# Inverse deviations by Newton steps, a normalization split between two engines, and three re-ordered steps in a four-layer graph kernel

## The chip, the cores and the metric

The kernel runs on one core of one Trainium2 chip, in a single launch. The metric is the device time of that launch in microseconds (us); lower is better. Only fp32 data takes part in the matrix products; the edge mask between layers is kept in bf16.

## The reference

Four graph layers follow each other on x (4096 x 256) and a weighted adjacency matrix adj (4096 x 4096). Every layer ends in the same residual normalization.

```python
def _layernorm(x, axis=-1, eps=1e-5):
    m = jnp.mean(x, axis=axis, keepdims=True)
    v = jnp.var(x, axis=axis, keepdims=True)
    return (x - m) / jnp.sqrt(v + eps)

x = _layernorm(x + L0(x, adj, adj, ...))   # 4-head attention, adj as bias and as mask
x = _layernorm(x + L1(x, adj, ...))        # graph attention: leaky_relu(e_src + e_dst), masked softmax, @ (x W)
x = _layernorm(x + L2(x, adj, ...))        # (D^-1/2 adj D^-1/2 x) W2^T + b2
x = _layernorm(x + L3(x, adj, ...))        # relu((D^-1/2 adj D^-1/2 x) W3)
```

The change touches how 1 / sqrt(v + eps) is formed after layer 0, how the last rows of layer 3 are normalized and stored, and the order of some steps at the start and the end of layer 0.

## The kernel before, in words

All stages stand in one function, `tile_gnn`, and nearly all of it is under a manual schedule: instructions of one engine run in the order in which the Python code issues them, and semaphores tie the engines together. So the order of the code is the order of each engine's queue. 128 rows make a chunk; there are 32 of them.

**Start of layer 0** (L709 to L734). SP and ScalarE issue the loads. SP: the first 512 columns of x transposed (`load_x(0)`, in two halves), `fetch` (what the first queries need), `load_x(1)`, four pieces of raw adjacency for `rows[0].load(0)`, four for `rows[0].load(1)`, then `load_x(2..4)`. ScalarE: weights and biases. `warm` (L209) keeps TensorE busy; `project_k(0)` (L215) makes the first 512 keys as two products, one per pair of heads, in the PSUM banks `po0` and `po1`, each summed over two halves of the feature axis (cc) and moved to SBUF by ScalarE (L228). `rows[0].begin("po1")` (L323) makes the first 128 queries in bank `po1`, and VectorE moves them (L338). Then `project_k(1)`, and the first masks: `make_bias` on VectorE turns raw adjacency (L287) and makes a bias of it (L292, L293). The first three of the steps below also carry the rest of the keys and values: `plan[t]` holds `project_v` (L235; its result lies in the PSUM tile `tr`, moved by VectorE at L248), `project_k` and `first_bias`.

**Layer 0, step by step** (`step(t)`, L501). A unit is one pair of heads of one row chunk: 64 units of NS = 4 steps, each step 1024 keys wide. In a step TensorE does the scores of step t into the two PSUM tiles `sc[0]`, `sc[1]` (L383); VectorE adds the bias, takes the maximum and writes z (L392); ScalarE makes exponentials four steps later (L408); TensorE turns them into the PSUM tile `tr` (L422); ScalarE copies them out (L430, in the last steps half of them by VectorE at L428); TensorE multiplies by the values (L440). `sc` and `tr` are single-buffered, so the next scores wait for L392 and the next turning waits for the copy. At a unit's end VectorE scales (`scale`, L491) with a row that went through a DRAM round trip on GpSimd's queue (`sums` L463, `spread` L484), or, for the last unit, through TensorE (L474); `finish` (L348) multiplies by the output weights (L352), adds the residual (L362) and takes the row statistics (L117, L118).

**The tail of layer 0** is hung on the last steps by the table `tail` (L663), n0 being the step eight before the end of the scores (nd). At n0 + 2 `ln_rstd(0, 30)` (L120) forms the inverse deviations of the 30 finished chunks: VectorE adds eps, ScalarE takes Sqrt, VectorE takes the reciprocal. `norm_part(j)` (L606) normalizes the j-th eighth of the rows on VectorE (L126) and stores it with a DMA of GpSimd's queue (L612). `turn_part(j)` (L616) turns an eighth of x with eight transposes into `sc[0]` and `sc[1]` (L622) and copies each out, cc = 0 by ScalarE (L625) if `split`, else by VectorE (L627). `project_ed` (L630) and `project_w` (L134) make the projections of layer 1. At nd + 7 `last_rstd` (L650) does the last two chunks.

**Layers 1 to 3.** Layer 1 (`gat_step`, L915) multiplies at L891. Layers 2 and 3 share `Block`: seven products per pair of chunks (L1059) in place of eight. The very last block ends in `end` (L1116): eight row groups n = 0 to 7 in two halves h of NSJ = 4; `weigh` multiplies by the weights (L1090), `onto_x` applies Relu on ScalarE (L1142) and adds to x (L1144; GpSimd for n = 0 to 4 and 6, VectorE for 5 and 7), `stats` takes the statistics on VectorE, and `put(h)` (L1151) forms the inverse deviations of the half, normalizes its four groups and stores them with two DMAs. `put(0)` stands before the loop over n = 4 to 7, so its four normalizations come ahead of that loop's VectorE work.

Of the kernel before, what the change touches and what calls it, by code (L numbers as in the profile page):

```python
# [9 lines left out]
BF16 = mybir.dt.bfloat16  # L10
AF = mybir.ActivationFunctionType
# [5 lines left out]
P = 128  # L17
# [19 lines left out]
EPS = 1e-5  # L37
WARM = 8
# [7 lines left out]
def tile_gnn(  # L46
# [38 lines left out]
    sel = const.tile([P, NCH], F32, name="sel")  # L85

# [38 lines left out]
    def ln_apply(dst, src, ci, engine=nc.vector):  # L125
        engine.tensor_scalar(  # L126
            dst, src, mv[:, ci, 0:1], rstd[:, ci : ci + 1], ALU.subtract, ALU.mult
        )
# [43 lines left out]
    with ExitStack() as l0:  # L172
# [42 lines left out]
        def project_k(mb):  # L215

            xt = x_in[mb]
            for pr in range(2):
                pk = ps_o.tile([P, 512], F32, tag=f"po{pr}", name="pk")
                for cc in range(2):  # L220
                    nc.tensor.matmul(  # L221
                        pk,
                        wkv_sb[:, cc, pr * P : (pr + 1) * P],
                        xt[:, cc, :],
                        start=(cc == 0),
                        stop=(cc == 1),
                    )
                nc.scalar.activation(  # L228
                    kT[:, pr, mb * 512 : (mb + 1) * 512],
                    pk,  # L230
                    AF.Identity,
                    bias=bqk_sb[:, 2 + pr : 3 + pr],
                )
# [23 lines left out]
        class Rows:  # L257
# [65 lines left out]
            def begin(self, tag):  # L323
                self.qT = wk2.tile([P, 2, P], F32, tag="qT", name="qT")
                pq = ps_o.tile([P, 512], F32, tag=tag, name="pq")
                for pr in range(2):
                    for cc in range(2):
                        for j in range(2):
                            h = 2 * pr + j
                            nc.tensor.matmul(  # L330
                                pq[j * HD : (j + 1) * HD, pr * P : (pr + 1) * P],
                                wq_sb[:, cc, h * HD : (h + 1) * HD],
                                self.xq[:, cc, :],
                                start=(cc == 0),
                                stop=(cc == 1),
                            )
# [164 lines left out]
        def step(t):  # L501
# [33 lines left out]
            if grow:  # L535
                if pr == 1 and k == NS - 3:
                    rows[ib + 1].begin(tag_o if attends else "po1")
# [77 lines left out]

        def turn_part(j, split=False):  # L616
            xs = parts.pop(j)
            xt = zp.tile([P, 2, NSB, NA, QB], F32, tag="z", name="xt1")
            for cc in range(2):
                px = sc[cc][:, 0:512].rearrange("p (a i) -> p a i", i=P)  # L620
                for a in range(NA):
                    nc.tensor.transpose(px[:, a, :], xs[:, a, cc * P : (cc + 1) * P], ident)  # L622
                to, px = xt[:, cc, :, :, :], px.rearrange("p a (b r) -> p b a r", r=QB)
                if split and cc == 0:
                    nc.scalar.copy(to, px)  # L625
                else:
                    nc.vector.tensor_copy(to, px)  # L627
            turned_x[j] = xt
# [21 lines left out]
        def last_rstd():  # L650
# [15 lines left out]
            n0 + 2: [(load_part, 2), (weight, 1, 1), (ln_rstd, 0, NCH - 2)],  # L666
# [9 lines left out]
            nd + 5: [(turn_part, 5, True)],  # L676
# [32 lines left out]
        with tc.manual_schedule():  # L709
# [11 lines left out]
            nc.scalar.dma_start(bv_b, bv.partition_broadcast(P))  # L721
            rows[0].load(1)
            for mb in range(2, 5):
# [5 lines left out]
            rows[0].begin("po1")  # L729
# [270 lines left out]
    with ExitStack() as l2:  # L1000
# [31 lines left out]
        class Block:  # L1032
# [83 lines left out]
            def end(self, t0):  # L1116
# [7 lines left out]
                py = {}  # L1124

# [25 lines left out]
                def put(h, engines):  # L1151
                    c0 = h * NP + self.jb * NSJ
                    ln_rstd(c0, c0 + NSJ)
                    ob = wk.tile([P, NSJ, D], F32, tag="ob", name="ob", bufs=2)
                    for s in (0, 1, 3, 2):
                        ln_apply(ob[:, s, :], xc[:, c0 + s, :], c0 + s, engines[s])
                    for s, queue in ((0, nc.sync), (2, (nc.sync, nc.scalar)[h])):
                        queue.dma_start(
                            out[(c0 + s) * P : (c0 + s + 2) * P, :].rearrange(
                                "(s p) e -> p s e", p=P  # L1160
                            ),
                            ob[:, s : s + 2, :],
                        )

# [24 lines left out]
                put(0, [nc.vector] * NSJ)  # L1189
# [6 lines left out]
                put(1, [nc.vector] * (NSJ - 1) + [nc.gpsimd])  # L1196
# [114 lines left out]
```

## Time and profile before

| what | value |
|---|---|
| time of the launch, median of 3 runs | 2694.16 us (2693.48 to 2695.2) |
| the profiled execution: its own time | 2693.25 us |
| its span, first to last instruction | 2691.5 us |
| TensorE clock granted, mean | 0.999 |
| TensorE busy | 2670.8 us |
| VectorE busy | 2189.5 us |
| ScalarE busy | 1638.3 us |
| GpSimd busy | 384.2 us |
| DMA | 312.31 MB, mean 116 GB/s |

Busy time by stretch of the span, in us:

| stretch | TensorE | VectorE | ScalarE | GpSimd |
|---|---|---|---|---|
| 0 to 75, start of layer 0 | 71.68 | 42.96 | 23.45 | 10.95 |
| 75 to 1300, layer 0 | 1224.80 | 1112.49 | 1171.47 | 325.01 |
| 1300 to 1345, its last steps | 42.87 | 34.14 | 40.37 | 10.61 |
| 1345 to 1410, into layer 1 | 60.55 | 43.73 | 42.46 | 6.20 |
| 1410 to 1858, layer 1 | 447.85 | 383.22 | 297.83 | 3.28 |
| 1858 to 2672, layers 2 and 3 | 813.55 | 561.94 | 58.82 | 22.30 |
| 2672 to 2691.5, the end | 9.53 | 10.98 | 3.88 | 5.82 |

A timeline line of the profile reads: start in us from the span's start, time in us, engine, source line, operation, output<-input, shape, count; in square brackets the idle time of the engine just before it and what ended that. PE is TensorE's matrix products, PEld its weight loads, DVE VectorE, ACT ScalarE, POOL GpSimd, SP SyncE; a q behind an engine's name is its queue, that issues DMAs.

### The profile page before, as it was taken

The numbers are of one execution on the slowest core, as the hardware profiler recorded it, in microseconds if no ns is written. First come the engines' busy times: TensorE is split into PE (matmuls) and PEld (weight loads), VectorE is DVE, ScalarE is ACT, GpSimd is POOL, SyncE is SP. The second block draws the span as 40 slices with busy tenths as digits, with TensorE's granted clock in tenths as the row PEclk, the third lists the DMA queues.
The fourth block names the chain that finished last, engine by engine and source line by source line (L and its number), as shares of the span: only waits on it lengthen the run. The fifth ranks groups of instructions, "written<-read, shape, count | busy, mean of one in ns | idle before, by whom it ended". The sixth has DMA issues, their size and how long they took to land.

```text
span 2691.5 us, 59102 instructions
## 1 busy us (share of the span) xinstructions
PE 2670.8 (99%) x23858; PEld 1835.5 (68%) x23858; DVE 2189.5 (81%) x4122; ACT 1638.3 (61%) x2677; POOL 384.2 (14%) x665
## 2 busy tenths in 40 slices
PE   9999999999999999999999999999999999999998
PEld 5777777777777777777778888886444444444444
DVE  5999999999999999999769988886966578676675
ACT  2899999999999999999967666672100001000000
POOL 1232232232222222222200000001200000000000
PEclk9999999999999999999999999999999999999999
DMA  7444444444444444444372222222544545455543
GB/s 157 93 94 95 91 93 97 90 93 97 90 91 99 90 92 97 89 94 97 109 219 79 72 78 77 73 79 73 177 157 163 171 157 172 156 168 176 177 162 107
DMA packets 679699, 312.31 MB, mean 116 GB/s; under 512 B 553504, under 2 KB 584096, under 8 KB 679424
## 3 DMA queue, kind: packets, MB, share of 16 engines
q1 hardware_dynamic: 655968, 264.97, 39.1%
q0 software_dynamic: 21504, 41.98, 4.3%
q8 instruction: 187, 3.06, 0.5%
q10 hardware_dynamic: 1952, 1.58, 0.2%
q14 instruction: 88, 0.72, 0.1%
HBM read 262.34 MB, written 46.07 MB: 115 GB/s over the span
## 4 chain that ended last, share of the span: by engine, by line
PE 96%; issue 1%; DMA 1%; ACT 1%; DVE 1%; SPq 0%; POOL 0%; POOLq 0%; DVEq 0%; ACTq 0%
PE m L1059 29%; PE po L440 17%; PE sc L383 17%; PE po L891 17%; PE ptr L422 11%; PE py L1090 2%; PE pq L330 1%; PE pp L352 1%; PE pv L241 1%; PE pk L221 1%; DMA wkv_sb<-in_wqkv 0%; DMA x<-xs 0%; SPq L271 0%; DMA mk<-edge 0%; DMA xt<-in_xT 0%
## 5 line engine op out<-in xcount | busy, mean ns | idle before, releaser
L392 DVE CUSTOM_DVE_ANT_0 z<-sc,bias 128x1024 f32<-128x1024 f32 x512 | 606.1, 1221 | 46.8 <-PE sc L383 46.7
L408 ACT ACTIVATE z<-z,nm 128x1024 f32<-128x1024 f32 x512 | 590.4, 1153 | 0.0
L430 ACT COPY pt<-ptr 128x1024 f32<-128x1024 f32 x507 | 510.5, 1007 | 65.4 <-PE ptr L422 64.6
L440 PE MATMUL po<-pt,xc 128*64 128x128 f32 x8192 | 504.1, 276 | 0.5 <-DVE pt L428 0.5
L383 PE MATMUL sc<-store,qT 64*128 64x512 f32 x2048 | 502.8, 604 | 0.1
L440 PEld LDWEIGHTS po<-pt,xc 128*64 128x64 f32 x8192 | 442.1, 137 | 18.1 <-DVE pt L428 0.8
L891 PE MATMUL po<-store,pt 128*128 128x257 f32 x2048 | 445.6, 379 | 0.0
L422 PEld LDWEIGHTS ptr<-ident,z 64*128 64x128 f32 x8192 | 322.9, 138 | 179.6 <-issue 87.7
L891 PEld LDWEIGHTS po<-store,pt 128*128 128x128 f32 x2048 | 387.3, 189 | 57.6
L422 PE MATMUL ptr<-ident,z 64*128 64x64 f32 x8192 | 356.7, 225 | 3.5 <-ACT pt L430 2.0
L1059 PE MATMUL m<-asum,ysum 128*128 128x512 f32 x672 | 324.7, 592 | 0.0
L383 PEld LDWEIGHTS sc<-store,qT 64*128 64x128 f32 x2048 | 194.0, 188 | 115.5 <-issue 109.6
L1059 PEld LDWEIGHTS m<-asum,ysum 128*128 128x128 f32 x672 | 127.7, 190 | 160.3 <-issue 139.7
L310 POOL DMA_DIRECT2D edge<-mk x256 | 143.1, 559 | 556.1 <-ACT mk L304 540.0
L1023 DVE TENSOR_TENSOR asum<-a,a 128x512 f32<-128x512 f32 x128 | 88.1, 688 | 150.9 <-PE m L1059 150.9
L1059 PE MATMUL m<-asum,store 128*128 128x512 f32 x448 | 210.5, 592 | 0.0
L1059 PE MATMUL m<-a,ysum 128*128 128x512 f32 x448 | 210.5, 592 | 0.0
L293 DVE SCALAR_TENSOR_TENSOR bias<-rt,gb,u 128x512 f32<-128x512 f32 x256 | 194.2, 759 | 9.1
L881 DVE STREAM_TRANSPOSE pt<-z 128x1024 f32<-128x1024 f32 x128 | 158.0, 1236 | 39.5 <-PE po L891 38.3
L1065 ACT COPY e<-m 128x512 f32<-128x512 f32 x28 | 16.2, 585 | 277.4 <-PE m L1059 277.4
L287 DVE STREAM_TRANSPOSE rt<-raw 128x512 f32<-128x512 f32 x256 | 180.0, 703 | 5.1 <-DMA raw<-in_adjT 4.8
L304 ACT ACTIVATE mk<-rt 128x512 bf16<-128x512 f32 x256 | 158.0, 617 | 6.5 <-DMA edge<-mk 3.5
(155 smaller groups left out, 2657.7 us busy)
## 6 DMA issues: line engine op xcount, KB each, us to landing
a<-in_adjT SPq DMA_DIRECT2D x256, 512.0 KB, 4.8
raw<-in_adjT SPq DMA_DIRECT2D x512, 128.0 KB, 3.9
edge<-mk POOLq DMA_DIRECT2D x256, 128.0 KB, 2.5
mk<-edge SPq DMA_DIRECT2D x256, 128.0 KB, 2.9
xq<-in_xT SPq DMA_DIRECT2D x32, 128.0 KB, 3.7
xr<-in_x SPq DMA_DIRECT2D x32, 128.0 KB, 3.0
x<-xs POOLq DMA_DIRECT2D x8, 512.0 KB, 6.5
xc<-x SPq DMA_DIRECT2D x8, 512.0 KB, 5.9
```

The costliest lines, as they stand in the source:

```text
L287: nc.vector.transpose(rt.rearrange("p (b r) -> p b r", r=QB), self.raw_now[:, half * nb : (half + 1) * nb, :],)
L293: nc.vector.scalar_tensor_tensor(self.bias[k][:, m0 : m0 + HT], rt, gb, u, ALU.mult, ALU.add)
L304: nc.scalar.activation(mk, rt, AF.Copy, accum_out=self.rs[:, j : j + 1])
L383: nc.tensor.matmul(ps[j][:, q * 512 : (q + 1) * 512], self.rows.qT[j * HD : (j + 1) * HD, self.pr, :], kT[j * HD : (j + 1) * HD, self.pr, ...
L392: nc.vector.tensor_tensor_reduce(z, ps[j], self.rows.bias[k], 1.0, NEG, ALU.add, ALU.max, self.mx[:, j, k : k + 1],)
L408: nc.scalar.activation(z, z, AF.Exp, bias=self.nm[:, j : j + 1], accum_out=self.ls[:, j, k : k + 1],)
L422: nc.tensor.transpose(pa[:, r, c, :], z[half, c * P : (c + 1) * P], ident[half, half])
L430: nc.scalar.copy(to, pa)
L440: nc.tensor.matmul(self.po[j * HD : (j + 1) * HD, 0:P], v_sb[:, ci, h * HD : (h + 1) * HD], self.pt[j][k][:, c, :], start=(ci == 0), stop= ...
L881: nc.vector.transpose(self.pt[:, :, s, :], self.z[s].rearrange("p (b r) -> p b r", r=QB))
L891: nc.tensor.matmul(self.po[:, 0 : D + 1], self.pt[:, b, :, :].rearrange("p s i -> p (s i)"), wh[:, b, :], start=(b == 0), stop=(b == NBK - 1),
L1059: nc.tensor.matmul(self.m[i], left, right, start=(c == 0), stop=(c == NP - 1))
```

## The change

The change has four parts.

1. **Start.** `project_k` takes both PSUM tiles at once, and for the first 512 keys sums the first half of the features for both pairs of heads before the second half. The first queries lie in `tr` instead of `po1`. `load_x(2)` is issued ahead of `rows[0].load(1)`.
2. **Newton.** For the 30 chunks at n0 + 2, ScalarE's Sqrt and VectorE's reciprocal give way to `ln_newton`: three VectorE instructions (eps, and a first guess made with integer arithmetic on the bits), then four Newton steps of four GpSimd instructions each, all on 128 x 30 values.
3. **Sixth part of x.** `turn_part(5, split)` at nd + 5 becomes two halves: cc = 0, copied by ScalarE, at nd + 4, and cc = 1, copied by VectorE, at nd + 6. Both come last in their step.
4. **End.** `put` is taken apart. `rates(h)` forms the inverse deviations and also -mean / deviation. Of half 0, groups 0, 1 and 3 are normalized by ScalarE (Identity with scale and bias) and group 2 by VectorE, after the loop over n = 4 to 7 instead of before it; of half 1, group 3 by ScalarE and 0 to 2 by VectorE. GpSimd normalizes nothing any more.

```diff
-    def ln_apply(dst, src, ci, engine=nc.vector):
-        engine.tensor_scalar(
+    def ln_newton(c0, c1):
+        n = c1 - c0
+        v, y = newton[:, 0, 0:n], rstd[:, c0:c1]
+        t = newton[:, 1, 0:n]
+        nc.vector.tensor_scalar(v, mv[:, c0:c1, 1], EPS, None, ALU.add)
+        nc.vector.tensor_scalar(
+            y.bitcast(I32), v.bitcast(I32), 1, None, ALU.arith_shift_right
+        )
+        nc.vector.tensor_scalar(
+            y.bitcast(I32), y.bitcast(I32), -1, MAGIC, ALU.mult, ALU.add
+        )
+        for _ in range(4):
+            nc.gpsimd.tensor_tensor(t, y, y, ALU.mult)
+            nc.gpsimd.tensor_tensor(t, t, v, ALU.mult)
+            nc.gpsimd.tensor_scalar(t, t, 0.5, 1.5, ALU.mult, ALU.subtract)
+            nc.gpsimd.tensor_tensor(y, y, t, ALU.mult)
+    def ln_apply(dst, src, ci):
+        nc.vector.tensor_scalar(
             dst, src, mv[:, ci, 0:1], rstd[:, ci : ci + 1], ALU.subtract, ALU.mult
...
+            pk = [ps_o.tile([P, 512], F32, tag=f"po{pr}", name="pk") for pr in range(2)]
+            both = [(pr, cc) for pr in range(2) for cc in range(2)]
+            for pr, cc in both if mb else sorted(both, key=lambda i: i[1]):
+                nc.tensor.matmul(
+                    pk[pr],
+                    wkv_sb[:, cc, pr * P : (pr + 1) * P],
+                    xt[:, cc, :],
+                    start=(cc == 0),
+                    stop=(cc == 1),
+                )
             for pr in range(2):
-                pk = ps_o.tile([P, 512], F32, tag=f"po{pr}", name="pk")
-                for cc in range(2):
-                    nc.tensor.matmul(
-                        pk,
-                        wkv_sb[:, cc, pr * P : (pr + 1) * P],
-                        xt[:, cc, :],
-                        start=(cc == 0),
-                        stop=(cc == 1),
-                    )
                 nc.scalar.activation(
                     kT[:, pr, mb * 512 : (mb + 1) * 512],
-                    pk,
+                    pk[pr],
                     AF.Identity,
                     bias=bqk_sb[:, 2 + pr : 3 + pr],
...
-            def begin(self, tag):
+            def begin(self, pq):
                 self.qT = wk2.tile([P, 2, P], F32, tag="qT", name="qT")
...
-                pq = ps_o.tile([P, 512], F32, tag=tag, name="pq")
...
-                    rows[ib + 1].begin(tag_o if attends else "po1")
+                    rows[ib + 1].begin(
+                        ps_o.tile([P, 512], F32, tag=tag_o if attends else "po1", name="pq")
+                    )
...
+        def turn_half(j, cc, by_act):
+            if cc == 0:
+                turned_x[j] = zp.tile([P, 2, NSB, NA, QB], F32, tag="z", name="xt1")
+            xs = parts.pop(j) if cc else parts[j]
+            px = sc[cc][:, 0:512].rearrange("p (a i) -> p a i", i=P)
+            for a in range(NA):
+                nc.tensor.transpose(px[:, a, :], xs[:, a, cc * P : (cc + 1) * P], ident)
+            to = turned_x[j][:, cc, :, :, :]
+            px = px.rearrange("p a (b r) -> p b a r", r=QB)
+            if by_act:
+                nc.scalar.copy(to, px)
+            else:
+                nc.vector.tensor_copy(to, px)
         def turn_part(j, split=False):
-            xs = parts.pop(j)
-            xt = zp.tile([P, 2, NSB, NA, QB], F32, tag="z", name="xt1")
             for cc in range(2):
-                px = sc[cc][:, 0:512].rearrange("p (a i) -> p a i", i=P)
-                for a in range(NA):
-                    nc.tensor.transpose(px[:, a, :], xs[:, a, cc * P : (cc + 1) * P], ident)
-                to, px = xt[:, cc, :, :, :], px.rearrange("p a (b r) -> p b a r", r=QB)
-                if split and cc == 0:
-                    nc.scalar.copy(to, px)
-                else:
-                    nc.vector.tensor_copy(to, px)
-            turned_x[j] = xt
+                turn_half(j, cc, split and cc == 0)
...
-            n0 + 2: [(load_part, 2), (weight, 1, 1), (ln_rstd, 0, NCH - 2)],
+            n0 + 2: [(load_part, 2), (weight, 1, 1), (ln_newton, 0, NCH - 2)],
...
-            nd + 5: [(turn_part, 5, True)],
+            nd + 4: [(turn_half, 5, 0, True)],
+            nd + 6: [(turn_half, 5, 1, False)],
...
+            load_x(2)
             rows[0].load(1)
-            for mb in range(2, 5):
+            for mb in range(3, 5):
                 load_x(mb)
             nc.scalar.dma_start(wout_sb, wout.rearrange("(c p) e -> p c e", p=P))
             nc.scalar.dma_start(bout_b, bout.partition_broadcast(P))
             warm()
             project_k(0)
-            rows[0].begin("po1")
+            rows[0].begin(ps_t.tile([P, TS], F32, tag="tr", name="pq"))
             project_k(1)
...
+                nmr = wk.tile([P, 2, NSJ], F32, tag="nmr", name="nmr", bufs=1)
+                obs = [wk.tile([P, NSJ, D], F32, tag="ob", name="ob", bufs=2) for h in range(2)]
...
-                def put(h, engines):
-                    c0 = h * NP + self.jb * NSJ
-                    ln_rstd(c0, c0 + NSJ)
-                    ob = wk.tile([P, NSJ, D], F32, tag="ob", name="ob", bufs=2)
-                    for s in (0, 1, 3, 2):
-                        ln_apply(ob[:, s, :], xc[:, c0 + s, :], c0 + s, engines[s])
-                    for s, queue in ((0, nc.sync), (2, (nc.sync, nc.scalar)[h])):
-                        queue.dma_start(
-                            out[(c0 + s) * P : (c0 + s + 2) * P, :].rearrange(
-                                "(s p) e -> p s e", p=P
-                            ),
-                            ob[:, s : s + 2, :],
+                def apply(h, s, by_act):
+                    ci = h * NP + self.jb * NSJ + s
+                    if by_act:
+                        nc.scalar.activation(
+                            obs[h][:, s, :],
+                            xc[:, ci, :],
+                            AF.Identity,
+                            bias=nmr[:, h, s : s + 1],
+                            scale=rstd[:, ci : ci + 1],
                         )
+                    else:
+                        ln_apply(obs[h][:, s, :], xc[:, ci, :], ci)
+                def put(h, s, queue):
+                    c0 = h * NP + self.jb * NSJ + s
+                    queue.dma_start(
+                        out[c0 * P : (c0 + 2) * P, :].rearrange("(s p) e -> p s e", p=P),
+                        obs[h][:, s : s + 2, :],
+                    )
+                def rates(h, between=()):
+                    cs = slice(h * NP + self.jb * NSJ, h * NP + (self.jb + 1) * NSJ)
+                    r = rstd[:, cs]
+                    nc.vector.tensor_scalar(r, mv[:, cs, 1], EPS, None, ALU.add)
+                    nc.scalar.activation(r, r, AF.Sqrt)
+                    for args in between:
+                        apply(*args)
+                    nc.vector.reciprocal(r, r)
+                    nc.vector.scalar_tensor_tensor(
+                        nmr[:, h, :], mv[:, cs, 0], -1.0, r, ALU.mult, ALU.mult
...
-                put(0, [nc.vector] * NSJ)
+                rates(0)
                 for n in range(NSJ, 2 * NSJ, 2):
                     for i in range(n, n + 2):
                         weigh(i, None, (1,))
                         onto_x(i)
                     stats(n)
                     stats(n + 1)
-                put(1, [nc.vector] * (NSJ - 1) + [nc.gpsimd])
+                apply(0, 0, True)
+                apply(0, 1, True)
+                put(0, 0, nc.sync)
+                rates(1, ((0, 2, False), (0, 3, True)))
+                put(0, 2, nc.sync)
+                for s in (3, 0, 1, 2):
+                    apply(1, s, s == 3)
+                put(1, 0, nc.sync)
+                put(1, 2, nc.scalar)
```

More of the change, by code (lines that the diff above doesn't have):

```diff
@@ L10 @@
 BF16 = mybir.dt.bfloat16
+I32 = mybir.dt.int32
 AF = mybir.ActivationFunctionType
@@ L37 @@
 EPS = 1e-5
+MAGIC = 0x5F3759DF
 WARM = 8
@@ L85, in tile_gnn @@
     sel = const.tile([P, NCH], F32, name="sel")
+    newton = const.tile([P, 2, NCH], F32, name="newton")
     x0_pre = dram.tile([N, D], F32, name="x0_pre")
@@ L1149, in stats @@
                     ln_stats(wk, xc[:, ci, :], ci)
-                def put(h, engines):
-                    c0 = h * NP + self.jb * NSJ
-                    ln_rstd(c0, c0 + NSJ)
-                    ob = wk.tile([P, NSJ, D], F32, tag="ob", name="ob", bufs=2)
-                    for s in (0, 1, 3, 2):
-                        ln_apply(ob[:, s, :], xc[:, c0 + s, :], c0 + s, engines[s])
-                    for s, queue in ((0, nc.sync), (2, (nc.sync, nc.scalar)[h])):
-                        queue.dma_start(
-                            out[(c0 + s) * P : (c0 + s + 2) * P, :].rearrange(
-                                "(s p) e -> p s e", p=P
-                            ),
-                            ob[:, s : s + 2, :],
-                        )
+                def apply(h, s, by_act):
[7 more added lines that the diff above has]
+                            scale=rstd[:, ci : ci + 1],
+                        )
+                    else:
[16 more added lines that the diff above has]
+                        nmr[:, h, :], mv[:, cs, 0], -1.0, r, ALU.mult, ALU.mult
+                    )
                 products(2)
```

## The prediction, on record before the run

> **What bounds the kernel now.** I read the page's busy times and its chain of waits first, then the chain in order of time, then the timeline of the four places that the change touches. From the page:
>
> ```profile
> span 2691.5 us, 59102 instructions
> ...
> PE 2670.8 (99%) x23858; PEld 1835.5 (68%) x23858; DVE 2189.5 (81%) x4122; ACT 1638.3 (61%) x2677; POOL 384.2 (14%) x665
> ...
> PE 96%; issue 1%; DMA 1%; ACT 1%; DVE 1%; SPq 0%; POOL 0%; POOLq 0%; DVEq 0%; ACTq 0%
> ```
>
> TensorE is the bound nearly everywhere, and the change takes no product away. It can only win where TensorE stands still or where the end hangs on other engines. The chain leaves TensorE in the first 21 us, around 1316 to 1321, 1366 to 1410, and after 2678. What is saved there goes through to the end, since TensorE's work from one place to the next stays.
>
> Start, from the timeline:
>
> ```profile
> 9.97 1.09 PE L330 MATMUL pq<-xq,w_sb 128*64 128x128 f32 x16 [0.78 <-ACT store L228]
> ...
> 16.55 0.71 DVE L287 STREAM_TRANSPOSE rt<-raw 128x512 f32<-128x512 f32 x1 [4.82 <-DMA raw<-in_adjT]
> ...
> 21.45 3.70 PE L221 MATMUL pk<-xt,wkv_sb 128*128 128x512 f32 x8 [1.18 <-DMA xt<-in_xT]
> ...
> 22.82 1.22 DVE L248 TENSOR_TENSOR xc<-pv,bv_b 128x1024 f32<-128x1024 f32 x1
> ...
> 24.99 3.62 PE L241 MATMUL pv<-wkv_sb,xt 128*128 128x256 f32 x16
> ```
>
> Read two queues here. TensorE waits for ScalarE before the first queries and for the third block of x at 21.45. VectorE waits for raw adjacency until 16.55 and is then busy without a gap until 24.04, when L248 has emptied `tr`; only then may the values at 24.99 be written.
>
> Newton's place (n0 + 2), same view:
>
> ```profile
> 1307.37 0.44 POOL L308 TENSOR_TENSOR mk<-mk,off_diag 128x128 bf16<-128x128 bf16 x1
> ...
> 1307.89 0.43 POOL L309 TENSOR_TENSOR mk<-mk,ident 128x128 bf16<-128x128 bf16 x1
> ...
> 1316.38 1.28 ACT L122 ACT_TABLE_LOAD   x1
> ...
> 1317.92 1.28 ACT L408 ACT_TABLE_LOAD   x1
> ...
> 1320.62 1.37 DVE L126 TENSOR_SCALAR xs<-xs,mv,rstd 128x256 f32<-128x256 f32 x4
> ...
> 1321.40 0.71 PE L422 MATMUL ptr<-ident,z 64*128 64x64 f32 x16 [1.99 <-ACT pt L430]
> ```
>
> Sqrt and the way back to Exp cost ScalarE two table loads; its copy L430 is late, and TensorE stands 1.99 us.
>
> The sixth part of x:
>
> ```profile
> 1366.36 1.96 PE L440 MATMUL po<-pt,xc 128*64 128x128 f32 x30 [0.54 <-DVE pt L428]
> ...
> 1369.99 0.28 DVE L491 TENSOR_TENSOR oT<-po,rb 128x128 f32<-128x128 f32 x1
> ...
> 1370.42 1.08 PE L352 MATMUL pp<-wout_sb,oT 128*64 128x256 f32 x8 [1.07 <-DVE rowsum L359]
> ```
>
> The last values are done at 1368.3, but the scaling L491 sits on VectorE behind the copy L627 (1369.38 to 1370.07), which itself waits for eight transposes.
>
> The end:
>
> ```profile
> 2685.86 0.17 DVE L121 TENSOR_SCALAR rstd<-mv 128x4 f32<-128x4 f32 x1
> ...
> 2686.59 1.39 POOL L126 TENSOR_SCALAR ob<-xc,mv,rstd 128x256 f32<-128x256 f32 x1 [4.04 <-DVE rstd L123]
> ...
> 2688.01 0.40 ACTq L1158 DMA_DIRECT2D out_x<-ob  x1
> ```
>
> GpSimd's 1.39 us normalization releases the last store; ahead of that, VectorE was the only engine with work.
>
> **What the Trainium skill says.** "ScalarE: Activation LUTs", What ACT_TABLE_LOAD costs, gives about 1283 ns for a load plus a drain of about 1380 ns. The trace agrees with the load (1.28 us) and shows no drain: Sqrt starts at 1317.67, as its load ends. The same page, Table sets, says that cheap functions (identity among them) are in every set, so ScalarE's Identity beside Sqrt and Relu at the end should load nothing; before, Relu and Sqrt alternate there without a load. "GPSIMD Engine Reference", Elementwise — side-by-side cycle accounting, has 2.6 cycles per element for a two-input operation; L1144 takes 0.725 us (median) for 256 values and L309 0.43 for 128, or 2.3 ns per value and about 0.14 us fixed (different types, so an estimate). "Perfetto Trace Analysis", GPSIMD Engine Instruction, advises start-to-start spacing for that engine: L308 to L309, which depends on it, is 0.52 us, 0.09 more than the duration.
>
> **Part 1, start.** The reordered first keys fill the waits for the second halves: eight passes of 0.427 us from 4.94 end at 8.35 instead of 9.20. The queries need not wait for ScalarE's second copy and follow at once, ending near 9.45 instead of 11.06; the next keys, scores and values come about 1.5 us earlier, and TensorE is ready for the third block at 18.75. That block is issued behind four raw pieces instead of eight: at 13.1 instead of 16.80. It took 4.6 us to land, so 17.7, or somewhat later behind raw pieces still under way. Its new place costs the four raw pieces of `rows[0].load(1)` one issue, 0.4 us on SP, then the sum is the same again; VectorE wants them only at 23.96, after issue near 17 plus 3.9 to 4.7. So TensorE does the third keys from 18.75 to 22.4, 2.7 us early. Then it runs into VectorE: raw adjacency lands as before, VectorE's work up to L248 is untouched, `tr` is free at 24.04 and the values start near 24.1 instead of 24.99. From there both engines go on as before, shifted. Putting the queries into `tr` adds a wait of the first values for L338, long past. **Gain 0.85 us**; bounds 0.4 and, if VectorE should not hold it, 2.6.
>
> **Part 2, Newton.** Removed: two loads, a Sqrt of 0.23 and a reciprocal of 0.34. Without them the copy L430 ends near 1318.6 and the transposes start at their beat, 4.80 us after those at 1314.54, at 1319.34: at most 2.06 us. Added: three VectorE instructions, 0.2 us each as L452 and L453 follow each other, from 1316.77, about as much as L121 and L123 with the wait took; L392 starts at 1317.4 instead of 1318.19. Then 16 dependent GpSimd instructions, from 1317.45. The trace has none of this kind. For 30 values: 0.14 + 30 x 0.0023 = 0.21 us, which the one-input copy L593 of 31 values (0.21) supports, plus 0.09 spacing: 0.30 each, 4.8 in all, done at 1322.25. Bounds: 0.21 each without spacing, 3.4; or the full 0.52 of 128 values, 8.3.
> Who waits: `norm_part(0)` at n0 + 3, and behind it on VectorE's queue the L392 pair of the next step, and on GpSimd the DMA of L612 and nothing urgent. L126 then runs 1322.25 to 1323.6, and the L392 pair (2.36 us, by the pair at 1312.26) to 1326.0. TensorE would like the following scores at 1324.7 (before: 1326.75). Its first head's passes go at once, the other head's at 1326.0; six of eight passes remain, 6/8 of 1.78, so the next transposes start at 1327.33 against 1328.53. **Gain 1.2 us**: the new wait eats 0.85 of the 2.06. Bounds +2.06 (Newton under 4.0) and -2.3 (8.3 us). Every further microsecond of Newton costs one.
>
> **Part 3, sixth part.** The first half's four transposes (half of 1.09, 0.55 us) come after the product L474, near 1365.4; there TensorE waits for L428 until 1366.36 after two passes of 0.43 in sum, so 0.55 + 0.43 just fits. ScalarE has been idle; its copy costs nothing, and its Sqrt load moves ahead too. L491 now follows the values at once: 1368.4 to 1368.7. The second half's transposes fill TensorE until 1368.8, L352 starts near 1368.9 instead of 1370.42. L627 (0.69) lies on VectorE from 1368.9, done before L362 is wanted at 1370.1. All that hangs on L362 (last normalization, projections) moves along. The store of the last rows moves too, and `load_rows` and later masks wait for it on SP; but those masks are first used near 1399 and land near 1389, so slow DMA is hidden by some 10 us. **Gain 1.5 us**; bounds 0.7 (the half doesn't fit its gap, DMA crowding) and 1.6.
>
> **Part 4, end.** Up to 2680.8 nothing changes but L123 followed by 0.2 for -mean / deviation. Then L1144 of group 5 need not wait behind four L126 (2680.82 to 2683.0): it goes when its Relu is done, near 2681.4. The statistics from 2681.8 take the 2.54 us that they took (2683.28 to 2685.82): 2684.36, 1.46 earlier. ScalarE does groups 0 and 1 meanwhile (0.48 each, by its Relu row), done at 2683.3. `rates(1)`: before, L121 to the first L126 took 0.65; with group 2 and the extra product between, 0.95. Three L126 on VectorE take 1.22: the last store goes 2.2 after L121, at 2686.55 instead of 2688.01. Three stores of 256 KB then follow closely; they move at 335 GB/s, 0.78 us each, the first from 0.8 after its issue at 2685.3: done at 2688.45, where before the two ended at 2689.85. **Gain 1.4 us**; bounds 0.8 and 1.6.
>
> **Sum.** 0.85 + 1.2 + 1.5 + 1.4 = 4.95 us. The profiled execution took 2693.25, 1.75 more than its span, so 2688.3 by its own count. It lies 0.9 below the median of the runs shown; against that median, 2694.16 - 4.95 = **2689.2 us**, 0.18% less.
>
> **Rivals.** (a) Newton is quick, under 4.0 us: 0.86 more, 2688.4. For it: the copy of 31 values; against: the spacing. (b) VectorE doesn't hold the start: 1.8 more, 2687.4. For it: TensorE's early readiness; against: no gap on VectorE between 16.55 and 24.04. (c) A small GpSimd operation costs the 0.52 of L308: Newton 8.3 us, 3.5 later, 2692.7. (d) **Slower:** a GpSimd instruction costs the same whatever its width, twelve at the 0.82 mean of L774 and four like L126's 1.39, each plus 0.09: 16.8 us, 12.0 later, with VectorE and then the scores held: 2701.2. The change as a whole stops winning when Newton takes 9.75 us, 0.61 per instruction. Against it: L593 at 0.21. That an edit does nothing (part 3's gap too short, part 1 hidden) is in the bounds.
>
> **How the numbers follow.** Likeliest 0.62 (2688.2 to 2690.4), a 0.16, b 0.06, c 0.11, d 0.05. A measurement here tells about 0.2% (5.4 us) from no change, so faster means under 2688.8: all of b, nearly all of a and under a third of the likeliest, 0.38. Slower than 2699.5 is most of d, 0.04. The rest, 0.58, is same. The range leaves out d and c's slow end above, and b's best case below: 2687.1 to 2691.7.
>
> **What would show it.** Right: no ACT table load near 1316; sixteen short GpSimd instructions ending about 4.8 us after VectorE's third; L126 waiting for them and scores a little late once; values at start near 24.1 with `tr` as the wait; L491 within 0.2 of the last values; the last store about 2.2 after the last `rates`. Wrong: GpSimd instructions over 0.45 us, a table load at the end, or TensorE waiting behind the first half's transposes.

## The result, and the profile after

| | before | after |
|---|---|---|
| time of the launch, median of 22 runs each | 2693.7 us (2693.03 to 2696.06) | 2689.74 us (2689.09 to 2692.57) |
| ratio, 95% interval | 1 | 0.9985 [0.9978, 0.9992] |
| the profiled execution: time, span | 2693.25, 2691.5 us | 2690.29, 2688.3 us |

The change takes off 3.96 us, 0.15%: within the 0.2% that the prediction counted as no change. It forecast 4.95 us and 2689.2.

The page of the changed kernel shows the same bound: TensorE's work is what it was; GpSimd has 15 instructions more, Newton's 16 less the normalization that it lost.

```profile
span 2688.3 us, 59124 instructions
...
PE 2672.3 (99%) x23858; PEld 1835.9 (68%) x23858; DVE 2188.3 (81%) x4122; ACT 1637.5 (61%) x2678; POOL 387.3 (14%) x680
...
PE 96%; DVE 1%; DMA 1%; ACT 1%; issue 0%; POOL 0%; SPq 0%; DVEq 0%; POOLq 0%; ACTq 0%
```

**The start**, timeline of after. The third keys (19.70) wait for nothing; TensorE now waits 1.34 us for VectorE's L272, which empties `tr`. But raw adjacency landed 0.54 us later than in before's profile (17.09 against 16.55), so this execution shows only 0.35 us of the gain (24.64 against 24.99).

```profile
17.09 0.71 DVE L311 STREAM_TRANSPOSE rt<-raw 128x512 f32<-128x512 f32 x1 [5.76 <-DMA raw<-in_adjT]
...
19.70 3.60 PE L244 MATMUL pk<-xt,wkv_sb 128*128 128x512 f32 x8
...
23.37 1.22 DVE L272 TENSOR_TENSOR xc<-pv,bv_b 128x1024 f32<-128x1024 f32 x1
...
24.64 3.72 PE L265 MATMUL pv<-wkv_sb,xt 128*128 128x256 f32 x16 [1.34 <-DVE xc L272]
```

**Newton**, timeline of after at n0 + 2. No table load is left, but the chain of 16 instructions lasts from 1317.27 to 1322.80. Read the third line of the first step: L144, with an immediate subtraction, takes 0.37 us, and the next instruction starts 0.46 after it, where the others follow at 0.31 to 0.34. VectorE waits 3.14 us for the last step, and TensorE's scores then wait for VectorE, the first head's until 1325.42 and the second head's weights until 1326.56.

```profile
1317.27 0.23 POOL L142 TENSOR_TENSOR newton<-rstd 128x30 f32<-128x30 f32 x1 [0.34 <-DVE rstd L138]
1317.58 0.25 POOL L143 TENSOR_TENSOR newton<-newton 128x30 f32<-128x30 f32 x1
1317.92 0.37 POOL L144 TENSOR_SCALAR newton<-newton 128x30 f32<-128x30 f32 x1
1318.38 0.25 POOL L145 TENSOR_TENSOR rstd<-rstd,newton 128x30 f32<-128x30 f32 x1
...
1322.55 0.25 POOL L145 TENSOR_TENSOR rstd<-rstd,newton 128x30 f32<-128x30 f32 x1
1322.84 1.38 DVE L148 TENSOR_SCALAR xs<-xs,mv,rstd 128x256 f32<-128x256 f32 x4 [3.14 <-POOL rstd L145]
...
1325.42 2.69 PE L406 MATMUL sc<-store,qT 64*128 64x512 f32 x7 [0.86 <-DVE mx L415]
...
1326.56 0.30 PEld L406 LDWEIGHTS sc<-store,qT 64*128 64x128 f32 x4 [0.85 <-DVE mx L415]
...
1327.95 0.59 PE L406 MATMUL sc<-store,qT 64*128 64x512 f32 x1
1327.96 1.07 PE L445 MATMUL ptr<-ident,z 64*128 64x64 f32 x13
```

**The sixth part of x.** The first half's transposes (1365.14) fit into the wait for L451; the scaling L514 comes at 1368.21, right after the values.

```profile
1365.14 0.60 PE L648 MATMUL sc<-ident,xs 128*128 128x128 f32 x4
...
1365.67 2.50 PE L463 MATMUL po<-pt,xc 128*64 128x128 f32 x32
...
1368.21 0.29 DVE L514 TENSOR_TENSOR oT<-po,rb 128x128 f32<-128x128 f32 x1 [1.85 <-PE po L463]
...
1368.68 1.08 PE L375 MATMUL pp<-wout_sb,oT 128*64 128x256 f32 x8
```

**The end.** The second half's `rates` come at 2682.79, 4.36 us after the first half's (before: 5.70), and the last store is issued 1.86 us later. ScalarE's Identity loads no table between the Relus and Sqrts, as "ScalarE: Activation LUTs", Table sets, says.

```profile
2680.41 1.08 ACT L1188 ACTIVATE ob<-xc,nmr,rstd 128x256 f32<-128x256 f32 x2
...
2682.79 0.17 DVE L1209 TENSOR_SCALAR rstd<-mv 128x4 f32<-128x4 f32 x1
...
2684.65 0.40 ACTq L1200 DMA_DIRECT2D out_x<-ob  x1
```

### The profile page after: what moved, and what is told of

Read it like the earlier page. It is cut to its first block, busy times and chain, and to the rows that moved or that the text cites. A ratio compares the mean times of both kernels' runs of the same rounds, so it can differ in the third digit from the quotient of the medians.

```text
span 2688.3 us, 59124 instructions
## 1 busy us (share of the span) xinstructions
PE 2672.3 (99%) x23858; PEld 1835.9 (68%) x23858; DVE 2188.3 (81%) x4122; ACT 1637.5 (61%) x2678; POOL 387.3 (14%) x680
## 3 DMA queue, kind: packets, MB, share of 16 engines
q10 hardware_dynamic: 1952, 1.58, 0.2%
## 4 chain that ended last, share of the span: by engine, by line
PE 96%; DVE 1%; DMA 1%; ACT 1%; issue 0%; POOL 0%; SPq 0%; DVEq 0%; POOLq 0%; ACTq 0%
PE m L1091 29%; PE po L463 18%; PE po L923 17%; PE sc L406 17%; PE ptr L445 11%; PE py L1122 2%; PE pp L375 1%; PE pq L353 1%; PE pv L265 1%; PE pk L244 1%; DMA wkv_sb<-in_wqkv 0%; DMA raw<-in_adjT 0%; PE sc L162 0%; DMA norm<-lt 0%; DVE pt L451 0%
```

## The experiments

After the result the theory was: parts 1, 3 and 4 brought what was forecast, and part 2 nothing, because Newton was too long for its place. The rival: all parts fell a little short, or raw adjacency's late landing was a cost of part 1.

One table serves all experiments. The three stages are read from each kernel's timeline: the **start**, from the first transpose of raw adjacency to the second values (L265; L241 in before); the **tail**, from the exponentials' transposes at n0 + 2 (1314.54 in before) to the last unit's output product (L375; L352), which holds parts 2 and 3; the **end**, from layer 3's first product of `end` to the issue of the last store. A stage doesn't depend on when data arrived before it, so it tells parts of 1 us apart where times scatter by 2 us. But each stage is read from one execution, and the start still holds a wait for the third block of x: in the four kernels with nothing of part 1 (before, e2, e3, e4) it lasts 8.44 to 9.16, and e3's 9.16 has a wait of 1.95 us where before has 1.18. The gain of part 1 is counted against before's 8.44, the shortest. "Before" was measured in each group of kernels: 2693.37 us with e1 to e4, 2694.46 with e5 to e8, 2693.89 with e9 to e12.

| kernel | start | tail | end | span | time, median | ratio to before |
|---|---|---|---|---|---|---|
| before | 8.44 | 55.88 | 15.27 | 2691.5 | as above | 1 |
| after | 7.55 | 54.46 | 13.65 | 2688.3 | 2689.74 | 0.9985 [0.9978, 0.9992] |
| e1, part 1 alone | 7.55 | 57.51 | 15.26 | 2691.7 | 2692.92 | 0.9996 [0.9988, 1.0005] |
| e2, part 2 alone | 8.48 | 55.82 | 15.26 | 2691.8 | 2693.6 | 1.0 [0.9992, 1.0008] |
| e3, part 3 alone | 9.16 | 54.30 | 15.26 | 2690.5 | 2693.08 | 0.9995 [0.9987, 1.0003] |
| e4, part 4 alone | 8.61 | 55.88 | 13.65 | 2690.0 | 2692.93 | 0.9996 [0.9988, 1.0004] |
| e5, all but part 2 | 7.55 | 54.29 | 13.65 | 2687.3 | 2690.09 | 0.9984 [0.9978, 0.9991] |
| e6, three Newton steps | 7.55 | 52.60 | 13.63 | 2685.8 | 2687.71 | 0.9979 [0.9971, 0.9987] |
| e7, Newton a step earlier | 7.55 | 52.24 | 13.64 | 2685.7 | 2687.69 | 0.9977 [0.9969, 0.9986] |
| e8, six Newton steps | 7.55 | 59.38 | 13.64 | 2693.2 | 2694.66 | 1.0002 [0.9994, 1.001] |
| e9, third block alone | 7.63 | 57.57 | 15.27 | 2691.9 | 2693.76 | 0.9999 [0.9991, 1.0008] |
| e10, rest of part 1 | 10.04 | 57.54 | 15.27 | 2694.3 | 2694.78 | 1.0001 [0.9993, 1.0009] |
| e11, early, three steps, added | 7.56 | 52.24 | 13.64 | 2685.3 | 2687.57 | 0.9977 [0.9968, 0.9987] |
| e12, constant added | 7.56 | 53.75 | 13.64 | 2687.5 | 2689.58 | 0.9985 [0.9979, 0.9992] |

### Each part alone (e1 to e4), and all but Newton (e5)

e1 puts part 1 alone into the kernel before.

```diff
+            load_x(2)
             rows[0].load(1)
-            for mb in range(2, 5):
+            for mb in range(3, 5):
...
-            rows[0].begin("po1")
+            rows[0].begin(ps_t.tile([P, TS], F32, tag="tr", name="pq"))
```

> Part 1 alone on the kernel before. Theory (VectorE holds the start, and the profiled run of the change only had a late landing of a weight load that neither kernel places differently): 0.85 us less than before, the second values at start some 24.1 after raw adjacency lands near 16.5, that is 7.55 after VectorE's first raw transpose. Rival (the change itself delays raw adjacency, as the 17.09 against 16.55 of its profile suggests): about 0.3 us less, with raw adjacency late by 0.5 again.

What lands late in the change's profile is raw adjacency (17.09), not a weight.

e2 puts part 2 alone into it.

```diff
-            n0 + 2: [(load_part, 2), (weight, 1, 1), (ln_rstd, 0, NCH - 2)],
+            n0 + 2: [(load_part, 2), (weight, 1, 1), (ln_newton, 0, NCH - 2)],
```

> Part 2 alone on the kernel before. Theory (Newton's 5.5 us wait on VectorE gives back all that the two table loads cost): between 0.4 less and 0.3 more than before, near 0.1 more. Rival (the forecast's size, 0.30 per GpSimd instruction, was right and other things hid it): 1.2 us less.

e3, part 3 alone.

```diff
-            nd + 5: [(turn_part, 5, True)],
+            nd + 4: [(turn_half, 5, 0, True)],
+            nd + 6: [(turn_half, 5, 1, False)],
```

> Part 3 alone on the kernel before. Theory: 1.6 us less, the scaling of the last unit within 0.1 of the last values, and the whole shift still there at layer 1's first product. Rival (DMA on the way into layer 1 takes it back): under 0.8 less.

e4, part 4 alone: the new `end` in the kernel before.

```diff
-                put(0, [nc.vector] * NSJ)
+                rates(0)
...
-                put(1, [nc.vector] * (NSJ - 1) + [nc.gpsimd])
+                rates(1, ((0, 2, False), (0, 3, True)))
```

> Part 4 alone on the kernel before. Theory: 1.5 us less, with the last store issued some 1.6 earlier. Rival (three stores of 256 KB in a row wait for each other): 0.8 less.

e5, the change with the old `ln_rstd` put back.

```diff
-            n0 + 2: [(load_part, 2), (weight, 1, 1), (ln_newton, 0, NCH - 2)],
+            n0 + 2: [(load_part, 2), (weight, 1, 1), (ln_rstd, 0, NCH - 2)],
```

> The change without part 2 (parts 1, 3 and 4, Sqrt and its table loads as before). Theory (Newton nets nothing): 3.9 us less than the kernel before, the same as the change within 0.3. Rival (Newton brings the forecast's 1.2): 2.8 less than before, 1.2 slower than the change.

The times of e1 to e4 decide nothing: each interval is 0.16 or 0.17% wide, over 4 us, and holds 1. The stages tell more. e1's start is 0.89 shorter, e3's tail 1.58, e4's end 1.62 (of which its span keeps some 1.4: the time after the last store's issue grew from 3.5 to 3.7 us), e2's tail 0.06. The end lasts 13.63 to 13.65 in all eight kernels that have part 4 and 15.26 or 15.27 in the other six. e5, with everything but Newton, has a tail 0.17 shorter than the change's; its time can't tell 1.2 us, but the tail can. So part 2 brings no time in its stage, and in the stages the rival of many small shortfalls falls.

The launches of e1 to e4 don't show as much as the stages do. To take out a fall of the clock, told next, compare only launches whose mean granted clock was 0.999, with those of before in the same group. Their medians are 0.5 us less for e1, 0.8 more for e2, 1.1 less for e3, 0.8 less for e4: each is 0.4 to 0.9 short of its stage. Later kernels come nearer: e5, e6, e7 and e11 gain 3.7, 5.7, 5.8 and 5.6, where their stages sum to 3.9, 5.6, 5.9 and 5.9; but e9 gains 0.2 of 0.8, and e12 3.7 of 4.4. These are 5 to 15 launches of each kernel, and why most fall short of their stages is not shown.

e1's tail, though, is 1.63 **longer** than before's, though nothing in it was changed. Its timeline and stretches (columns: length, busy PE, PEld, DVE, ACT, POOL, granted clock, DMA) show why:

```profile
1319.97 1.09 PE L423 MATMUL ptr<-ident,z 64*128 64x64 f32 x16 [2.00 <-ACT pt L431]
1320.84 3.24 PE L384 MATMUL sc<-store,qT 64*128 64x512 f32 x8
```

```profile
1320.00:1322.00 2.00, 2.00 (x20) 1.49 (x22) 0.55 (x2) 1.91 (x3) 0.81 (x1) 0.51 0.00 0
1322.00:1324.00 2.00, 2.00 (x12) 0.71 (x10) 0.00 (x0) 1.30 (x3) 0.00 (x0) 0.64 0.76 262
```

and the stretch of the kernel before that follows the same stall:

```profile
1322.00:1324.00 2.00, 2.00 (x22) 0.99 (x20) 0.08 (x1) 2.00 (x4) 0.81 (x1) 1.00 0.17 59
```

TensorE stood for the two table loads as in before (2.00 us against 1.99). In e1 the granted clock then fell to 0.51 and the scores took 3.24 us instead of 1.94; in before it stayed at 1.00. The last section counts how often.

### Which piece of part 1 does it (e9, e10)

e9 moves only the third block of x.

```diff
+            load_x(2)
             rows[0].load(1)
-            for mb in range(2, 5):
+            for mb in range(3, 5):
```

> The kernel before with one line of part 1 alone: the third block of x is issued ahead of the pieces of row 1's edges. Theory: VectorE alone sets the start, and the second values wait for the raw adjacency and the third keys; with the third block here early the third keys follow the second ones at once, so that measured from the first raw transpose the second values start about 7.6 us later instead of 8.44, the whole 0.85 to 0.9 us of part 1. Time: 0.9 us less than before. Rival: TensorE's queries also have to move, since they stand ahead of the keys; then this alone gives less than half of it, 0.4 us or less.

e10 has the other two edits of part 1.

```diff
+            for pr, cc in both if mb else sorted(both, key=lambda i: i[1]):
...
-            rows[0].begin("po1")
+            rows[0].begin(ps_t.tile([P, TS], F32, tag="tr", name="pq"))
```

> The kernel before with the rest of part 1: the order of the first keys' passes and the first queries in the transposes' bank, the third block left where it was. Theory: nothing, within 0.2 us, because the third block still lands late and VectorE's transposes of the raw adjacency stand between; the second values start 8.3 to 8.5 us after the first raw transpose, as before. Rival: the bank was what held the start, and this gives 0.4 us or more.

In e9 the start takes 7.63 us, 0.81 less than in before, as the theory said; the rival falls. Its time is not 0.9 less but the same. The profiled run lost 1.69 us in the tail, as e1's did, but the lost clock doesn't explain all: 8 of its 13 launches have it, and 22 of the 46 of before. e10's timeline:

```profile
16.16 0.71 DVE L289 STREAM_TRANSPOSE rt<-raw 128x512 f32<-128x512 f32 x1 [5.75 <-DMA raw<-in_adjT]
...
20.97 5.40 PE L222 MATMUL pk<-xt,wkv_sb 128*128 128x512 f32 x8 [2.01 <-DMA xt<-in_xT]
...
26.20 3.62 PE L243 MATMUL pv<-wkv_sb,xt 128*128 128x256 f32 x16
```

```profile
22.00:24.00 2.00, 2.00 (x4) 0.74 (x3) 2.00 (x4) 0.59 (x1) 0.00 (x0) 0.60 1.15 302
```

TensorE was ready earlier and so stood 2.01 us for the third block instead of 1.18. Then its clock fell to 0.60 and, in the next 2 us, 0.55, and the third keys took 5.40 us, not 3.60. With keys of 3.60 us the values would have come some 8.2 us after the transpose (an estimate: 10.04 less 1.80), near what was expected. So the third block's place is nearly the whole gain of part 1, 0.81 of 0.89; its other two edits gain nothing that this one execution shows, and here TensorE only waited longer.

### How long Newton may be (e6, e7, e8, e11, e12)

e6: three steps. The constant is added there instead of subtracted, because each subtracting step turns the sign of y, and three would leave it negative.

```diff
-        for _ in range(4):
+        for _ in range(3):
...
-            nc.gpsimd.tensor_scalar(t, t, 0.5, 1.5, ALU.mult, ALU.subtract)
+            nc.gpsimd.tensor_scalar(t, t, -0.5, 1.5, ALU.mult, ALU.add)
```

> The change with three Newton steps in place of four, at the same place. Theory (a microsecond of Newton is a microsecond of TensorE while VectorE waits): one step is 1.39 us in the trace, so 1.4 us less than the change, 5.3 less than before. Rival (the delay after the wait has another cause): no more than 0.3 less than the change.

e7: the four steps of the change, issued one tail entry earlier.

```diff
-            n0 + 1: [(load_part, 1), (weight, 0, 1)],
-            n0 + 2: [(load_part, 2), (weight, 1, 1), (ln_newton, 0, NCH - 2)],
+            n0 + 1: [(load_part, 1), (weight, 0, 1), (ln_newton, 0, NCH - 2)],
+            n0 + 2: [(load_part, 2), (weight, 1, 1)],
```

> The change with all four Newton steps one step of the loop earlier (n0 + 1), with the same number of instructions. Theory (only the place of the wait costs; the statistics of the 30 chunks are there by then): the wait before the first normalization shrinks to under 0.6 us and the whole 2.06 of the table loads comes in, 2.0 to 2.2 us less than the change, 6 less than before. Rival (sixteen GpSimd instructions cost as such, [...]by pushing back the DMAs of GpSimd's queue): under 0.8 less than the change.

e8: six steps.

```diff
-        for _ in range(4):
+        for _ in range(6):
```

> The change with six Newton steps in place of four. Theory: two steps of 1.39, so 2.8 us more than the change, 1.2 less than before. Rival (part of Newton is hidden, so more steps cost less than their length): under 1.5 more than the change.

e12: four steps in the adding form, in the change's place.

```diff
-            nc.gpsimd.tensor_scalar(t, t, 0.5, 1.5, ALU.mult, ALU.subtract)
+            nc.gpsimd.tensor_scalar(t, t, -0.5, 1.5, ALU.mult, ALU.add)
```

> The change with one instruction of each Newton step in another form: t times -0.5 plus 1.5 instead of t times 0.5 minus 1.5, four steps, same place. Theory: the subtracting form is what makes the step long (0.33 to 0.37 us against 0.22 in the run with three steps), so that Newton ends some 0.4 to 0.5 us sooner, in 5.1 instead of 5.53, and the time is 0.4 us less than the change. Rival: the forms cost the same and the run with three steps gained by its missing step alone; then Newton takes 5.5 us and the time is the change's.

e11: e7's place, three steps, the adding form.

```diff
-        for _ in range(4):
+        for _ in range(3):
...
-            nc.gpsimd.tensor_scalar(t, t, 0.5, 1.5, ALU.mult, ALU.subtract)
+            nc.gpsimd.tensor_scalar(t, t, -0.5, 1.5, ALU.mult, ALU.add)
...
-            n0 + 1: [(load_part, 1), (weight, 0, 1)],
-            n0 + 2: [(load_part, 2), (weight, 1, 1), (ln_newton, 0, NCH - 2)],
+            n0 + 1: [(load_part, 1), (weight, 0, 1), (ln_newton, 0, NCH - 2)],
+            n0 + 2: [(load_part, 2), (weight, 1, 1)],
```

> The change with Newton's steps issued one tail entry earlier, at the first entry, with three steps instead of four and the constant added instead of subtracted (what the earlier two runs changed singly). Theory: VectorE's wait for Newton is gone already by the earlier issue alone, so that fewer steps add nothing: 2.0 to 2.2 us less than the change, 6 less than before, the same as the earlier issue alone within 0.3. Rival: GpSimd's steps take time from VectorE even where nothing waits for them; then some 0.3 to 0.5 us less than the earlier issue alone.

Newton's end is counted here from the transposes at n0 + 2, and the gain of part 2 is the tail of e3 (54.30, part 3 with the old deviation), or of before for e2, less the kernel's own tail:

| kernel | Newton, us | its end after the transposes | gain of part 2 |
|---|---|---|---|
| after | 5.53 | 8.58 | -0.16 |
| e2 | 5.55 | 8.37 | 0.06 |
| e12 | 5.06 | 7.87 | 0.55 |
| e6 | 3.79 | 6.73 | 1.70 |
| e7 | 5.59 | 4.53 | 2.06 |
| e11 | 4.05 | 3.72 | 2.06 |
| e8 | 8.31 | 11.37 | -5.08 |

From after to e12 Newton ends 0.71 us sooner and the tail gains 0.71; from e12 to e6 1.14 and 1.15. So in this stretch each microsecond of Newton costs one, as the prediction said, and Newton breaks even with the table loads when it ends some 8.4 us after the transposes. e12's first lines show the form's price, 0.22 us where the change has 0.33 to 0.37, and what is left of the two waits:

```profile
1317.58 0.22 POOL L144 TENSOR_SCALAR newton<-newton 128x30 f32<-128x30 f32 x1
...
1322.01 1.38 DVE L148 TENSOR_SCALAR xs<-xs,mv,rstd 128x256 f32<-128x256 f32 x4 [2.67 <-POOL rstd L145]
...
1324.59 1.84 PE L406 MATMUL sc<-store,qT 64*128 64x512 f32 x4 [0.16 <-DVE mx L415]
```

e12's own time (2689.58) is 0.16 below the change's, not the 0.4 expected, with intervals that overlap nearly wholly; only the trace tells them apart. e6, of which 1.4 was expected, gave 1.86 in its tail, because it had the cheaper form (0.71, by e12) as well as a step less (1.15).

In e7's timeline both waits are gone, and Newton lies in a stretch in which nobody asks for it:

```profile
1319.01 1.38 DVE L148 TENSOR_SCALAR xs<-xs,mv,rstd 128x256 f32<-128x256 f32 x4
...
1324.04 1.94 PE L406 MATMUL sc<-store,qT 64*128 64x512 f32 x8
```

It gains the full 2.06, the table loads' whole stall; the time is 2.05 below the change's, which was measured in another group. e11 adds nothing to that (2687.57 against 2687.69), as its theory said. Both, and e6, beat the kernel before by 6.3 to 6.8 us (each against the runs of before in its group) and the change's median by 2.0 to 2.2.

e8 lost more than its longer Newton: its tail is 4.92 longer than the change's for a Newton that ends 2.79 later. Its timeline has TensorE idle for 3.63 us, and from 1326 to 1334 the granted clock was 0.66, 0.50, 0.50 and 0.64.

```profile
1325.30 1.38 DVE L148 TENSOR_SCALAR xs<-xs,mv,rstd 128x256 f32<-128x256 f32 x4 [5.92 <-POOL rstd L145]
...
1327.87 4.07 PE L406 MATMUL sc<-store,qT 64*128 64x512 f32 x7 [3.63 <-DVE mx L415]
```

## Why the prediction was nearly right, point by point

- **What bounds.** Right: TensorE's work is unchanged (23858 products before and after), and everything won lies in its idle times and at the end.
- **Part 1, 0.85: right.** VectorE sets the start; the stage is 0.89 shorter. The values were forecast near 24.1 with raw adjacency at 16.55; it came 0.54 later, and they came at 24.64. That lateness is not the change's: other kernels with the same loads in the same order (e1, e5 to e8, e11, e12) have it between 15.96 and 16.90, and the mean of all eight, 16.51, is that of before and e2 to e4, 16.52. A detail failed in this execution, without harm: eight first key passes at 0.427 should have ended at 8.35, but they ended at 9.64 (4.71 us together; in before 4.26), so that the queries came 0.4 us earlier, not 1.5. In e5 to e7, with the same order, they took 3.60 us and ended near 8.4, as forecast; what holds them elsewhere is not shown. VectorE's work covered it.
- **Part 2, 1.2: the term that failed.** The step was "0.14 + 30 x 0.0023 = 0.21 us ... plus 0.09 spacing: 0.30 each, 4.8 in all". Tensor with tensor held, 0.31 to 0.34 from start to start. Tensor with two immediates, of which the profile before had no row, took 0.41 to 0.46 in the subtracting form, and Newton 5.53. With a start 0.14 later than forecast it ended 8.58 us after the transposes instead of 7.71: 0.87 us. The rest, 0.49, is the next step: "six of eight passes remain, 6/8 of 1.78". That took the passes for one row of eight. But the two heads' passes run side by side: in before's records the eight start in four pairs (1321.95 and 1321.96, 1322.44 twice, 1322.87 twice, 1323.30 twice); in after two start alone (1325.42, 1325.95), two pairs follow (1326.56, 1327.10), then two alone (1327.52, 1327.95). That is two streams of four, the second begun late, so the first head's two passes that went ahead saved nothing for the second head. From the second head's release (weights at 1326.56) to the end of the last pass (1327.95 + 0.59) it is 1.98 us, as long as all eight take in one piece (1.94), and 13 of the 16 transposes come only after that pass has started. A whole 1.78 in place of 6/8 of it is 0.45 more. 0.87 + 0.49 = 1.36, the difference between 1.2 and -0.16. The price per further microsecond was right, and so was the 2.06 of the table loads (e7).
- **Part 3, 1.5: right**, 1.58; the half just fits its gap, and layer 1 starts earlier by as much as L375 does (1.74 in after): no transfer takes it back. From that product to layer 3's `end` it is 1302.32 us in before and in after.
- **Part 4, 1.4: right**, some 1.4 in the span.
- **Sum.** 0.89 - 0.16 + 1.58 + 1.4 = 3.7 us by stages; 3.96 in the medians, 3.2 in the two profiled spans (the late adjacency). The forecast gain was 0.99 larger than that of the medians. The forecast time was off by only 0.54, because the reference median, 2694.16 from 3 runs, lay 0.46 above that of the 22: that is luck. A part of the 3.96 seems to be luck too: the prediction has no term for the clock, and the change lost it in 3 of 22 launches, before in 64 of 136 (last section). Among launches at 0.999 alone, the change's 19 have a median of 2689.69 and the 72 of before in the later groups 2693.1: 3.4 us, or 3.6 in their spans (2687.7 against 2691.3). The two differ since the change's launches outlast their spans by 1.97 us in the mean and before's by 1.79; why is open.
- **Rivals.** (a) and (b) didn't come; (c) gave 2692.7 for a Newton of 8.3 us; e8 has that length and took 2694.66, and its clock fell as well; (d) fell with 0.23 to 0.37 us per instruction.

## What to carry to other kernels

A chain of small dependent instructions is priced by its start-to-start spacing in its own form, and then by where its result is first wanted: a step earlier was worth 2 us here, and a whole Newton step fewer nothing on top. Where times scatter by more than the edit is worth, measure the stage between two events that the edit encloses, in several kernels, and name the event that moved; then see whether the launches agree, for a stage comes from one execution. And an idle time of TensorE of 2 us could cost twice here, once as idle and once in the clock after it.

## What was not expected of the hardware

**The clock after a short idle.** The launch's mean granted clock, 0.998 or 0.999, tells the two outcomes of the stall apart: of the 14 profiled executions the four at 0.998 (e1, e8, e9, e10) all show the fall after 1318 and the ten at 0.999 show none. The mark doesn't say where a clock fell: e10's fell at the start too. By that mark the kernel before fell in 64 of its 136 runs (median 2695.2 us against 2693.1), and the six kernels that keep the old deviation (e1, e3, e4, e5, e9, e10; idle 1.99 to 2.00 us there) in 38 of 86; the kernels with Newton and an idle of 0.86 us at most (after, e2, e6, e7, e11, e12) in 12 of 92; e8, idle for 3.63, in 13 of 13. So with part 2 the fall is rarer, which its stage doesn't show. An estimate from these counts and the two medians of before is 2.1 us x (102/222 - 12/92), 0.7 us in the mean; in e2, part 2 alone, it doesn't come out as time, for its mean and that of before in its group are both 2693.83. The fall is also part of the scatter of e1, e3 and e4 (medians at 0.998 and at 0.999 lie 1.1 to 1.7 us apart). In its section Part 1: The HAM clock gate, "TensorE: Matmul & The Clock Gate" of the Trainium skill puts the fall after an idle window of about 3.4 us that runs freely; an idle time of 2.00 us can't hold such a window, wherever it lies, and yet it sufficed here in some executions and not in others. What tells them apart is open; no run here varied how the stall lies in time. Where the 12 runs of the kernels with little idle there lost their clock is open too.

**The same load, landing at different times.** Raw adjacency's first transpose came between 15.96 and 17.09 us in fourteen executions, though no edit changed what is queued ahead of it. It moves the values behind it by the same amount; no edit here was made to control it.
